# Row sums of the first triangle stage on ScalarE, and a new order of that stage's words

## The chip, the cores and the metric

The kernel runs on one core of a Trainium2 chip. A core has TensorE (PE, matrix products into PSUM; its weight loads are shown apart as PEld), VectorE (DVE), ScalarE (ACT), GpSimd (POOL) and SyncE (SP, which here only issues transfers). Each engine takes its instructions in program order and waits for semaphores of the others. The metric is the time on the device in microseconds (us); less is better. Two times of this kernel that lie within about 0.2% of each other can't be told apart.

## The reference, cut to what matters

```python
# x: 4 images of 64 x 64 x 256, fp32
f, g, v = xt @ Wf + bf, xt @ Wg + bg, xt @ Wh + bh          # layer 0: attention over 4096 positions
beta = softmax(einsum('bqd,bkd->bqk', g, f), axis=-1)
x = x + (einsum('bqk,bkd->bqd', beta, v) @ Wo + bo)
q, k, v1, v2 = (x @ W for W in (Wq, Wk, Wv1, Wv2))          # layer 1: triangle attention, 8 heads of 32
scores = einsum('bilhd,bljhd->biljh', q, k) / sqrt(32)
att = softmax(scores, axis=2)                               # over l
out = einsum('biljh,bilhd,bljhd->bijhd', att, v1, v2)
h = layer_norm(x + out @ Wo)
out = layer_norm(relu(h @ W1 + b1) @ W2 + b2 + h)
```

The change concerns one thing in it: for the first image, the denominators of the second softmax, which are sums of exp(scores) over l.

## The kernel before, in words

The four images go one after the other, each through an attention stage (`layer0`) and a triangle stage. For images 1 to 3 the triangle stage (`next_layer1`) also carries the layer norms and the MLP of the image before. For image 0 there is no image before, so its triangle stage (`first_layer1`) carries other work: the projections of x of the other three images (24 slices of 512 positions, class `Ahead`) and half of its own v1 and v2 projections (class `Late`). The change touches only this first triangle stage.

**A step.** The stage has 32 steps: 4 pairs of heads, and for each pair 8 groups of 8 rows i. `scores` and `take_scores` make, for a whole pair, the tile S of exp(scores), 128 partitions (head, j) by 64 rows i by 64 values l. Then, for each step:

- `sums` (L967 and L969 on DVE): the sum over l of each of the step's 8 rows of 64 values, one TENSOR_REDUCE of 128x512 into 8 columns of `dens`, and the reciprocal of these into `rd`.
- `weights` (L977, ACT): 8 multiplications of a row by its reciprocal, into `es`.
- `turn_weights` (L994, PE): four 128x128 transposes into a PSUM tile `att`. The 8 matrices of 128x64 that this gives are the step's 8 *products*.
- `copy_weights` (L1002, ACT): the last 2 or 3 of these 8 matrices into SBUF as `attP`, for GpSimd.
- `product` (L1042): `att` times v2, 128x2048 values. The last `npool(step)` products go to GpSimd (`Rp`, two buffers), the others to DVE, which reads `att` in PSUM (`R`, three buffers).
- `accumulate` (L1052, PE): sums a product over l with v1 as the weights, eight instructions of 128x512 in four column groups, into a PSUM tile `acc`. Only when it has run is the product's buffer free.
- `take` (L1062, ACT) copies `acc` out, and `store` (L1071, SP) issues eight transfers per step.
- `stationary` (L1021, ACT): v1 into the weight tile `wsel`, of which there are two.

**The order.** Nothing schedules this at run time: the order is written out by hand as a list of words, ORDER0, which is run through once for each *period* (11 periods, of which 1 to 9 hold products). One period does four steps. A word is a letter, the step within the four (and for some letters the product or half), and after the slash how many periods late it is: in period p, `R25/2` is product 5 of step 4(p-2)+2. The words: S sums, W weights, t and c transposes and copy for GpSimd, R product, A accumulate, T take (and store), V stationary; sp, sf scores; e, f exp of scores; v, u, g, a, b the projections for the other images (v and g on PE, u and a on ACT, b on DVE); m, n, o, p the own late projections (m and o on PE, n and p on ACT). A word only puts instructions into an engine's queue, so the list fixes the order on each engine, and the engines slip against each other as far as buffers allow.

A slice s of the projections ahead is loaded by SP (`xT`, L377) when both words v and g of slice s-2 have been issued. When four products of steps 24 to 29 have been issued, GpSimd issues transfers that spread gT and fT for the next image's attention (L278, L284).

`npool(step)` is 2 for every fourth step (step % 4 == 3) and 3 for the others: 11 of a period's 32 products for GpSimd, 88 of 256 in the stage.

Of the kernel before, what the change touches and what calls it, by code (L numbers as in the profile page):

```python
# [14 lines left out]
AF = mybir.ActivationFunctionType  # L15
ALU = mybir.AluOpType
AX = mybir.AxisListType
# [8 lines left out]
IG = 8  # L26
NIG = N // IG
# [37 lines left out]


ORDER0 = """
    A21/2 g1/2 S3/1 W1/1 A27/2 A23/2 A26/2 a1/2 V3/2 A24/2 R32/2 b1/2 m1/2 T20/2 c3/2 t0/1 v2/2 n1/2 R25/2 A25/2
    R33/2 sp0/1 T21/2 A32/2 R34/2 R36/2 R30/2 A33/2 e00/1 u2/2 e01/1 o1/2 R31/2 g2/2 c0/1 R37/2 A34/2 A36/2
    A30/2 A31/2 A37/2 V0/1 R35/2 T30/2 t1/1 R00/1 p1/2 a2/2 b2/2 A35/2 R03/1 T31/2 sf0/1 A00/1 R02/1 g0/1 f0/1  # L70
    a0/1 b0/1 R05/1 f1/1 R07/1 A05/1 A03/1 v3/2 R06/1 u3/2 m0/1 S2/1 W2/1 c1/1 v0/1 V1/1 R01/1 A02/1 n0/1 R04/1
    A07/1 A01/1 A04/1 R12/1 u0/1 A06/1 T00/1 sp1/1 T01/1 R13/1 R15/1 R14/1 A13/1 e10/1 e11/1 t2/1 R10/1 A12/1
    R17/1 V2/1 A15/1 A14/1 A10/1 R16/1 R11/1 S0 R22/1 W3/1 g3/2 c2/1 W0 A17/1 R27/1 A11/1 v1/1 R20/1 a3/2 b3/2
    u1/1 o0/1 p0/1 S1 R21/1 T10/1 t3/1 A16/1 T11/1 A20/1 R23/1 A22/1 R24/1 R26/1
""".split()


@with_exitstack
def attention_then_triangle_kernel(
# [6 lines left out]
    nc = tc.nc  # L86
# [22 lines left out]
    def ctile(shape, name):  # L109
        return const.tile(shape, F32, tag=name, name=name)  # L110
# [100 lines left out]
    dens = ctile([P, 256 + 16], "dens")  # L211
# [130 lines left out]
    class Ahead:  # L342
        def __init__(self):
            shapes = {"x": [C, T], "v": [P, NKC, P], "gf": [8, P, 2, 2, P]}
            self.d = {
                b: {n: dram.tile(sh, F32, tag="ah" + n, name="ah" + n, bufs=NB) for n, sh in shapes.items()}
                for b in range(1, NB)
            }
            self.n = 8 * (NB - 1)
            self.raw, self.xT, self.vp, self.gf, self.t = {}, {}, {}, {}, {}  # L350
            self.parts = None
# [532 lines left out]
    class Layer1:  # L884
        def __init__(self, b, io, safe):
            self.b, self.io, self.safe = b, io, safe

            self.aT = dram.tile([C, 2, N // 2, N], F32, tag="aT", name="aT")
            io["a"] = self.aT
            self.S, self.v2, self.qk, self.v1, self.att, self.ao = {}, {}, {}, {}, {}, {}  # L890
            self.R, self.begun, self.acc, self.rec, self.e = {}, {}, {}, {}, {}
            self.owed = lambda: None

# [57 lines left out]
                )  # L953


        def sums(self, step):
            pair, ig = divmod(step, NIG)
            rows = self.S[pair][:, ts(ig, IG), :]
            if self.safe:
                nmx = small.tile([P, IG], F32, tag="mxl", name="mxl")  # L960
                nc.vector.tensor_reduce(nmx, rows, AX.X, ALU.max, negate=True)
                den = small.tile([P, IG], F32, tag="den", name="den")
                for i in range(IG):
                    nc.scalar.activation(rows[:, i, :], rows[:, i, :], AF.Exp, bias=nmx[:, i : i + 1])
            else:
                den = dens[:, ts(step, IG)]
            nc.vector.tensor_reduce(den, rows, AX.X, ALU.add)  # L967
            rec = small.tile([P, IG], F32, tag="rd", name="rd")
            nc.vector.reciprocal(rec, den)  # L969
            self.rec[step] = (rows, rec)  # L970
# [8 lines left out]

        def npool(self, step):  # L980
            if self.b == 0:
                return 2 if step % 4 == 3 else 3
            return 3 - step % 2


# [431 lines left out]
    def step_words(L, fetched, stored, spread, late=None):  # L1417
        made, taken, sps = {}, {}, {}

        def do(w, step, m):  # L1420
            if not 0 <= step < NSTEP:
                return
            if w == "R":
                if step not in made:
                    made[step] = 0
                    L.begin(step)
                L.product(step, m)
                made[step] += 1
                if made[step] == 4:
                    spread(step)  # L1430
                if made[step] == 8:
                    if step == 1:
                        L.fetch_v2(1)
                    if step == NIG - 1 and late is not None:
                        L.fetch_v2(2, 2)
                        late.room = True
                        late.fetch()
                    elif step in (NIG - 1, 2 * NIG - 1):
                        L.fetch_v2((step + 1) // NIG + 1)
                    fetched(step + 1)  # L1440
            elif w == "A":
                L.accumulate(step, m)
            elif w == "T":
                L.take(step, m)
                taken[step] = taken.get(step, 0) + 1
                if taken[step] == 2:
                    L.store(step)
                    stored(step)
            elif step == 0:
                return  # L1450
            elif w == "S":
                L.sums(step)
            elif w == "W":
                L.weights(step)
            elif w == "V":
                L.stationary(step)
                L.fetch_v1(step + 2)
            elif w == "t":
                L.turn_weights(step)
            elif w == "c":  # L1460
                L.copy_weights(step)


        def scores(j):
            if 0 <= j < 12:
                L.scores(1 + j // 4, j % 4)
                sps[j] = L.sp
                if j % 4 == 3 and j // 4 + 2 < NPAIR:
                    L.fetch_qk(j // 4 + 2)

        def take_scores(j, half):
            if 0 <= j < 12:
                L.sp = sps[j]
                L.take_scores(half)

        L.fetch_v1(2)
        return do, scores, take_scores

    def words_of(order):
        for w in order:  # L1480
            w, late = (w.split("/") + ["0"])[:2]
            yield w, int(late)

    def first_layer1(L, ahead, F):
        used = {}

        def fetched(step):
            if 24 <= step < 31:
                ahead.fetch(F, 1, step)

        own = Late(L)
        step_word, scores, take_scores = step_words(
            L, fetched, lambda step: None, lambda step: ahead.spread(F, 1, step), own
        )

        def front_word(w, s, cc):
            if not 0 <= s < ahead.n:
                return
            if w in "vg":
                used[s] = used.get(s, 0) + 1  # L1500
            if w == "v":
                ahead.values(s)
            elif w == "u":
                ahead.valued(s)
            elif w == "g":
                ahead.factors(s)
            elif w == "a":
                ahead.factored(s)
            elif w == "b":
                ahead.parted(s)  # L1510
            if w in "vg" and used[s] == 2:
                ahead.load(s + 2)

        for period in range(NSTEP // 4 + 3):
            if period == 1:
                L.owed()
            for word, late in words_of(ORDER0):
                i, last = period - late, int(word[-1])
                if word[0:2] == "sp":
                    if 2 * i + last > 0:  # L1520
                        scores(2 * i + last)
                elif word[0] == "e":
                    if 2 * i + int(word[1]) > 0:
                        take_scores(2 * i + int(word[1]), last)
                elif word[0:2] == "sf":
                    if i == 0:
                        scores(0)
                elif word[0] == "f":
                    if i == 0:
                        take_scores(0, last)  # L1530
                elif word[0] in "RATSWVtc":
                    step_word(word[0], 4 * i + int(word[1]), last)
                elif word[0] in "mnop":
                    if 0 <= i < 4:
                        own.word(word[0], 2 * i + last)
                elif 0 <= i < 4 and int(word[1]) < 2:
                    front_word(word[0], 2 * i + int(word[1]), last)
                elif 4 <= i < 8:
                    front_word(word[0], 4 * i - 8 + int(word[1]), last)
        ahead.fetch(F, 1, NSTEP)  # L1540
# [193 lines left out]
```

## Time and profile before

| what | value |
|---|---|
| median of 3 runs | 3623.9 us (3619.18 to 3624.72) |
| profiled execution | 3623.49 us; span 3621.6 us |
| PE busy in the span | 3516.2 us, 97% |
| DVE busy | 2849.8 us, 79% |
| ACT busy | 1923.5 us, 53% |
| POOL busy | 1777.1 us, 49% |
| first triangle stage, from its first product to the next image's first scores on PE | 443.5 to 872.2 us of the span |

The page divides the span into 40 slices of 90.5 us, and gives the busy share of each engine in tenths; the first triangle stage is slices 5 to 9 or so, counted from 0. Groups of instructions are given with a line, an engine, what they write and read with the shapes, a count, and then the busy time, the mean length of one in ns, and the idle time just before them with what ended it.

### The profile page before, as it was taken

The page shows a single profiled execution, that of the slowest core. Times are in us where ns is not written, and L with a number is a line of the kernel's source. Part 1 is how long each engine was busy: PE and PEld are TensorE (multiplying, and loading weights), DVE is VectorE, ACT ScalarE, POOL GpSimd, SP SyncE. Part 2 cuts the span into 40 slices and gives each one's busy share as a digit, 9 for nine tenths or more (in the row PEclk, how much of TensorE's full clock was granted, in tenths as well). Part 3 has the DMA queues.
Part 4 walks back from the last instruction along what each step waited for, and adds up shares of the span by engine and source line. Part 5 has one row for each costly group of instructions (what it writes and reads, how often), then busy time and mean ns, then how long its engine had stood idle before and what let it go on. Part 6 is the DMA issues. An engine that isn't in the chain of part 4 may idle for free.

```text
span 3621.6 us, 58681 instructions
## 1 busy us (share of the span) xinstructions
PE 3516.2 (97%) x22218; PEld 1887.8 (52%) x22218; DVE 2849.8 (79%) x2662; ACT 1923.5 (53%) x4221; POOL 1777.1 (49%) x904
## 2 busy tenths in 40 slices
PE   9999999988999999999999999999999999999998
PEld 6555444434555555554455555555355555555477
DVE  4777499996555569999777749999787766999987
ACT  3444455544444366665444446666444446777655
POOL 5000099995000058899111118989611116999920
PEclk9999999999999999999999999999999999999999
DMA  9444555456111264426322254343633335441221
GB/s 174 137 132 125 138 151 133 126 132 139 47 50 50 81 153 102 108 62 114 96 95 88 82 141 117 83 104 79 131 93 99 96 108 142 96 94 49 66 69 57
DMA packets 509492, 374.37 MB, mean 103 GB/s; under 512 B 320080, under 2 KB 450896, under 8 KB 500368
## 3 DMA queue, kind: packets, MB, share of 16 engines
q1 hardware_dynamic: 460160, 343.56, 34.7%
q0 software_dynamic: 36160, 19.94, 5.5%
q10 hardware_dynamic: 12880, 7.01, 0.7%
q8 instruction: 178, 2.92, 0.3%
q14 instruction: 114, 0.93, 0.1%
HBM read 205.73 MB, written 164.63 MB: 102 GB/s over the span
## 4 chain that ended last, share of the span: by engine, by line
PE 68%; POOL 7%; DVE 6%; issue 4%; ACT 2%; DMA 0%; SPq 0%; ACTq 0%; DVEq 0%; POOLq 0%
PE o L590 18%; PE acc L1052 17%; PE proj L673 6%; POOL Rp L1042 6%; PE s L563 5%; PE mp L1303 5%; PE zp L1323 5%; PE sp L940 3%; DVE R L1042 3%; PE v1p L705 2%; PE hp L1160 2%; PE y L642 1%; PE att L994 1%; PE htp L1270 1%; PE hp L1166 0%
## 5 line engine op out<-in xcount | busy, mean ns | idle before, releaser
L1042 POOL TENSOR_TENSOR Rp<-attP,v 128x2048 f32<-128x2048 f32 x328 | 1491.3, 4579 | 410.4 <-ACT attP L1002 367.3
L1042 DVE TENSOR_TENSOR R<-att,v 128x2048 f32<-128x2048 f32 x696 | 1545.9, 2277 | 70.4 <-PE acc L1052 51.8
L590 PE MATMUL o<-e,v 128*128 128x512 f32 x2048 | 1043.7, 592 | 0.0
L575 ACT ACTIVATE e<-s 128x1024 f32<-128x1024 f32 x512 | 522.9, 1023 | 532.4 <-PE s L563 447.6
L597 DVE TENSOR_TENSOR esum<-esum,e 128x2048 f32<-128x2048 f32 x224 | 511.8, 2285 | 369.9 <-ACT e L575 367.9
L563 PE MATMUL s<-gT,fT 128*128 128x512 f32 x1024 | 786.5, 770 | 8.8 <-ACT e L575 4.7
L1052 PE MATMUL acc<-R,wsel 128*32 128x512 f32 x5568 | 705.4, 602 | 27.7 <-DVE R L1042 20.4
L590 PEld LDWEIGHTS o<-e,v 128*128 128x128 f32 x2048 | 388.3, 190 | 276.7 <-issue 233.8
L1062 ACT COPY ao<-acc 128x1024 f32<-128x1024 f32 x256 | 256.3, 1012 | 291.5 <-PE acc L1052 203.3
L1052 PE MATMUL acc<-Rp,wsel 128*32 128x512 f32 x2624 | 345.5, 598 | 22.3 <-POOL Rp L1042 21.6
L1052 PEld LDWEIGHTS acc<-R,wsel 128*32 128x32 f32 x5568 | 155.4, 110 | 397.6 <-issue 277.4
L1337 POOL TENSOR_TENSOR hz<-hz,log_bc 128x512 f32<-128x512 f32 x32 | 45.6, 1426 | 599.9 <-ACT hz L1247 599.9
L563 PEld LDWEIGHTS s<-gT,fT 128*128 128x128 f32 x1024 | 194.4, 190 | 245.0 <-issue 231.9
L977 ACT ACTIVATE es<-S,rd 128x64 f32<-128x64 f32 x1024 | 258.3, 337 | 15.0 <-DVE rd L969 13.1
L1231 POOL TENSOR_SCALAR nt<-mv 128x2 f32<-128x2 f32 (+1 forms) x49 | 9.4, 191 | 505.1 <-DVE mv L1186 500.0
L1303 PE MATMUL mp<-hT,w 128*128 128x256 f32 x1024 | 244.7, 384 | 1.7 <-ACT hT L1275 1.7
L1323 PE MATMUL zp<-w,hid 128*128 128x256 f32 x1024 | 240.0, 385 | 2.5 <-ACT hid L1312 2.1
L1323 PEld LDWEIGHTS zp<-w,hid 128*128 128x128 f32 x1024 | 187.9, 190 | 50.1 <-issue 14.7
L1303 PEld LDWEIGHTS mp<-hT,w 128*128 128x128 f32 x1024 | 185.2, 190 | 54.7 <-ACT attP L1002 12.6
L619 DVE RECIPROCAL rec<-den 128x512 f32<-128x512 f32 x32 | 107.4, 3357 | 126.5 <-PE den L615 121.2
L1052 PEld LDWEIGHTS acc<-Rp,wsel 128*32 128x32 f32 x2624 | 80.9, 110 | 210.1 <-issue 143.6
L950 ACT ACTIVATE S<-sp 128x512 f32<-128x512 f32 x128 | 131.4, 1092 | 77.9 <-PE sp L940 77.9
(195 smaller groups left out, 3699.0 us busy)
## 6 DMA issues: line engine op xcount, KB each, us to landing
v<-v2d SPq DMA_DIRECT2D x44, 512.0 KB
v1c<-v1d SPq DMA_DIRECT2D x128, 128.0 KB
aT<-ao SPq DMA_DIRECT2D x1024, 16.0 KB
A<-aT SPq DMA_DIRECT2D x256, 64.0 KB
hz<-raw SPq DMA_DIRECT2D x32, 512.0 KB
y<-yT SPq DMA_DIRECT2D x56, 256.0 KB
q<-st SPq DMA_DIRECT2D x56, 256.0 KB
k<-st SPq DMA_DIRECT2D x52, 256.0 KB
```

The source lines that it names most:

```text
L563: nc.tensor.matmul(s_ps[r // 2][:, r % 2, :], fT[tt][:, ts(r * 4 + n, P)], gT[qb // 4][:, ts(qb % 4, QB)], start=True, stop=not safe,)
L575: nc.scalar.activation(e[g][:, 2 * j : 2 * j + 2, :], s_ps[j], AF.Exp)
L590: nc.tensor.matmul(o_ps[qb], F.v[tt][:, r * 4 + n, :], es[:, r, :], start=(k == 0 and r == 0), stop=(k == 7 and r == 3),)
L597: nc.vector.tensor_tensor(esum[qb], esum[qb], es, ALU.add)
L673: nc.tensor.matmul(ps, w[:, cc, rows], y(qb, cc), start=(cc == 0), stop=(cc == 1))
L950: nc.scalar.activation(self.S[pair][:, :, l0 : l0 + 8].rearrange("p i l -> p l i"), sp[:, lh], AF.Copy if self.safe else AF.Exp,)
L977: nc.scalar.mul(e[:, i, :], rows[:, i, :], rec[:, i : i + 1])
L1042: eng.tensor_tensor(R, src.unsqueeze(1).to_broadcast([P, D, N]), v2[h], ALU.mult)
L1052: nc.tensor.matmul(acc[32 * c : 32 * c + 32, n % 2, :], w[:, n, c, 16 * h : 16 * h + 32], R[:, ts(c, 8), :].rearrange("p d j -> p (d j)"), ...
L1062: nc.scalar.copy(self.ao[step][:, ts(np, 2)].rearrange("p k d j -> p k (d j)"), self.acc[step][np])
L1303: nc.tensor.matmul(self.mp[:, fc % 2, :], w1_sb[:, cc, ts(fc, P)], self.hT[tt][:, cc, :], start=(cc == 0), stop=(cc == 1),)
L1323: nc.tensor.matmul(zp[:, n, :], self.hid[tt][:, fc, ts(n, P)], w2_sb[:, fc, :], start=(fc == 0), stop=(fc == 3 and tt not in self.hT2),)
```

## The change

ScalarE adds up the rows: for each step from 1 on there is a new word K (`row_sums`), which runs eight activations of 128x64, each of which writes a row of S back onto itself with the identity function and puts the sum of the row into its column of `dens`. For these steps `sums` keeps only the reciprocal; step 0 is still added up by DVE, inside `layer0`. The number of products that GpSimd takes is read from a string of 32 digits, one for each step, and comes to 85 in place of 88. ORDER0 is replaced by another list.

```diff
 ORDER0 = """
-    A21/2 g1/2 S3/1 W1/1 A27/2 A23/2 A26/2 a1/2 V3/2 A24/2 R32/2 b1/2 m1/2 T20/2 c3/2 t0/1 v2/2 n1/2 R25/2 A25/2
-    R33/2 sp0/1 T21/2 A32/2 R34/2 R36/2 R30/2 A33/2 e00/1 u2/2 e01/1 o1/2 R31/2 g2/2 c0/1 R37/2 A34/2 A36/2
-    A30/2 A31/2 A37/2 V0/1 R35/2 T30/2 t1/1 R00/1 p1/2 a2/2 b2/2 A35/2 R03/1 T31/2 sf0/1 A00/1 R02/1 g0/1 f0/1
-    a0/1 b0/1 R05/1 f1/1 R07/1 A05/1 A03/1 v3/2 R06/1 u3/2 m0/1 S2/1 W2/1 c1/1 v0/1 V1/1 R01/1 A02/1 n0/1 R04/1
-    A07/1 A01/1 A04/1 R12/1 u0/1 A06/1 T00/1 sp1/1 T01/1 R13/1 R15/1 R14/1 A13/1 e10/1 e11/1 t2/1 R10/1 A12/1
-    R17/1 V2/1 A15/1 A14/1 A10/1 R16/1 R11/1 S0 R22/1 W3/1 g3/2 c2/1 W0 A17/1 R27/1 A11/1 v1/1 R20/1 a3/2 b3/2
-    u1/1 o0/1 p0/1 S1 R21/1 T10/1 t3/1 A16/1 T11/1 A20/1 R23/1 A22/1 R24/1 R26/1
+    A14/2 u1/2 A25/2 A15/2 T11/2 R26/2 A24/2 S1/1 R21/2 u2/2 R27/2 t3/2 R22/2 c3/2 m1/2 S0/1 A26/2 W0/1 A22/2
+    g1/2 A21/2 R36/2 g2/2 R23/2 A27/2 a2/2 n1/2 A23/2 R20/2 R34/2 a1/2 T21/2 A20/2 V3/2 sp0/1 T20/2 e01/1 R35/2
+    b1/2 A34/2 A36/2 R37/2 R31/2 e00/1 V0/1 t0/1 o1/2 v3/2 A31/2 R33/2 R32/2 R30/2 b2/2 A35/2 c0/1 A33/2 A32/2
+    A37/2 A30/2 p1/2 W1/1 T31/2 T30/2 v0/1 R03/1 sf0/1 R02/1 t1/1 R05/1 V1/1 u3/2 A03/1 g3/2 f0/1 f1/1 A02/1
+    R07/1 A05/1 o0/1 R01/1 K2/1 R06/1 A07/1 A01/1 u0/1 R00/1 A00/1 c1/1 a3/2 K3/1 p0/1 T00/1 R04/1 S2/1 g0/1
+    W2/1 R11/1 A04/1 A06/1 b3/2 sp1/1 a0/1 R10/1 T01/1 e11/1 R16/1 t2/1 R17/1 b0/1 A11/1 A10/1 R12/1 e10/1 A16/1
+    V2/1 c2/1 R13/1 A12/1 m0/1 v2/1 R15/1 S3/1 K1 A17/1 R14/1 A13/1 v1/1 n0/1 R25/1 T10/1 W3/1 R24/1 K0
 """.split()
+ON_POOL = "33233233323333322333323323232323"
...
+        def row_sums(self, step):
+            pair, ig = divmod(step, NIG)
+            if not self.safe:
+                for i in range(IG):
+                    row = self.S[pair][:, ig * IG + i, :]
+                    nc.scalar.activation(
+                        row, row, AF.Identity, accum_out=dens[:, step * IG + i : step * IG + i + 1]
+                    )
+                self.summed.add(step)
...
-            nc.vector.tensor_reduce(den, rows, AX.X, ALU.add)
+            if step not in self.summed:
+                nc.vector.tensor_reduce(den, rows, AX.X, ALU.add)
...
         def npool(self, step):
             if self.b == 0:
-                return 2 if step % 4 == 3 else 3
+                return int(ON_POOL[step])
             return 3 - step % 2
...
+            elif w == "K":
+                L.row_sums(step)
```

More of the change, by code (lines that the diff above doesn't have):

```diff
@@ L67 @@
 ORDER0 = """
-    A21/2 g1/2 S3/1 W1/1 A27/2 A23/2 A26/2 a1/2 V3/2 A24/2 R32/2 b1/2 m1/2 T20/2 c3/2 t0/1 v2/2 n1/2 R25/2 A25/2
-    R33/2 sp0/1 T21/2 A32/2 R34/2 R36/2 R30/2 A33/2 e00/1 u2/2 e01/1 o1/2 R31/2 g2/2 c0/1 R37/2 A34/2 A36/2
-    A30/2 A31/2 A37/2 V0/1 R35/2 T30/2 t1/1 R00/1 p1/2 a2/2 b2/2 A35/2 R03/1 T31/2 sf0/1 A00/1 R02/1 g0/1 f0/1
-    a0/1 b0/1 R05/1 f1/1 R07/1 A05/1 A03/1 v3/2 R06/1 u3/2 m0/1 S2/1 W2/1 c1/1 v0/1 V1/1 R01/1 A02/1 n0/1 R04/1
-    A07/1 A01/1 A04/1 R12/1 u0/1 A06/1 T00/1 sp1/1 T01/1 R13/1 R15/1 R14/1 A13/1 e10/1 e11/1 t2/1 R10/1 A12/1
-    R17/1 V2/1 A15/1 A14/1 A10/1 R16/1 R11/1 S0 R22/1 W3/1 g3/2 c2/1 W0 A17/1 R27/1 A11/1 v1/1 R20/1 a3/2 b3/2
-    u1/1 o0/1 p0/1 S1 R21/1 T10/1 t3/1 A16/1 T11/1 A20/1 R23/1 A22/1 R24/1 R26/1
+    A14/2 u1/2 A25/2 A15/2 T11/2 R26/2 A24/2 S1/1 R21/2 u2/2 R27/2 t3/2 R22/2 c3/2 m1/2 S0/1 A26/2 W0/1 A22/2
[5 more added lines that the diff above has]
+    V2/1 c2/1 R13/1 A12/1 m0/1 v2/1 R15/1 S3/1 K1 A17/1 R14/1 A13/1 v1/1 n0/1 R25/1 T10/1 W3/1 R24/1 K0
 """.split()
+ON_POOL = "33233233323322333323323323232323"
 @with_exitstack
@@ L892, in __init__ @@
             self.owed = lambda: None
+            self.summed = set()
         def fetch_qk(self, pair, first=False):
@@ L1530, in first_layer1 @@
                         take_scores(0, last)
-                elif word[0] in "RATSWVtc":
+                elif word[0] in "RATKSWVtc":
                     step_word(word[0], 4 * i + int(word[1]), last)
```

## The prediction

> **What bounds the kernel now.** The table of busy time comes first. PE is busy for 97% of the whole span, but the change touches one stage only, the first triangle stage, and an average over all stages does not say who sets the pace there. So I cut that stage into its periods of four steps, which the scores' matmuls mark (they begin at 540.70, 591.94 and 643.17 us, so a period lasts 51.2 us), and read the busy time of each engine per period. Columns: from and to, length, then busy us and count of PE, PEld, DVE, ACT, POOL, then PE's granted clock and the DMA share.
>
> ```profile
> 530.30:581.50 51.20, 48.78 (x544) 22.79 (x536) 50.35 (x34) 28.91 (x75) 49.94 (x12) 1.00 0.51 139
> ...
> 735.50:787.00 51.50, 43.90 (x454) 19.49 (x455) 50.83 (x37) 23.61 (x71) 51.34 (x16) 0.97 0.55 124
> 787.00:838.00 51.00, 44.57 (x449) 18.54 (x446) 47.97 (x32) 22.39 (x61) 50.96 (x19) 0.90 0.92 175
> 838.00:872.00 34.00, 27.41 (x288) 13.62 (x284) 23.80 (x16) 10.78 (x21) 26.85 (x10) 0.95 0.53 121
> ```
>
> DVE and POOL are both busy for 98% of a period; they share the products and bound the stage together. ACT is busy for 56%. PE's 48.8 us contain modelled ends; by the starts in the timeline a product's eight matmuls take 0.86 us, transposes 0.59, v 1.87, g 0.87, m 1.72, o 1.87, scores 1.9, and 32 products, 4 transposes and two each of the others make 46.3 us.
>
> Next the groups of this stage, for the length of one instruction (window 450 to 900 us, shapes kept apart).
>
> ```profile
> L1042 POOL TENSOR_TENSOR Rp<-attP,v 128x2048 f32<-128x2048 f32 x87 | 395.1, 4582 | 16.4 <-PE acc L1052 6.8 <-ACT attP L1002 5.5 <-issue 2.1
> L1042 DVE TENSOR_TENSOR R<-att,v 128x2048 f32<-128x2048 f32 x166 | 368.6, 2273 | 15.0 <-PE acc L1052 11.5 <-ACT attP L1002 3.5
> L977 ACT ACTIVATE es<-S,rd 128x64 f32<-128x64 f32 x240 | 60.7, 340 | 12.9 <-DVE rd L969 12.7
> L967 DVE TENSOR_REDUCE dens<-S 128x8 f32<-128x512 f32 x29 | 19.6, 674 | 0.0
> ```
>
> In a row these overlap a little: seven DVE products take 15.42 us, so one starts every 2.20; six on POOL take 27.25, one every 4.54; a sum starts 0.71 before its reciprocal; eight `es` rows take 2.02, one every 0.24. Both engines' idle time is small, and its largest piece is at the end of the stage, which the timeline of DVE and then PE shows.
>
> ```profile
> 849.99 2.29 DVE L1042 TENSOR_TENSOR R<-att,v 128x2048 f32<-128x2048 f32 x1 [6.58 <-PE acc L1052]
> ```
> ```profile
> 843.10 3.85 PE L383 MATMUL vp<-wh,xT 128*128 128x128 f32 x16 [4.53 <-DMA xT<-ahx]
> ...
> 868.24 1.07 PE L1052 MATMUL acc<-R,wsel 128*32 128x512 f32 x8
> 869.23 2.05 PE L383 MATMUL vp<-wh,xT 128*128 128x128 f32 x16
> 871.21 0.65 PE L251 MATMUL gf<-xT,wg 128*32 128x128 f32 x16
> ```
>
> PE waits for a slice xT, the accumulates behind it are late, DVE finds no free buffer for 6.6 us. After the last accumulate PE still has a v and a g, 3 us, before the next attention's scores at 872.22.
>
> **What the Trainium skill says.** *GPSIMD Engine Reference*, Engine selection, has GpSimd about twice as slow as VectorE on elementwise operations of two inputs; the trace agrees (4582 against 2273 ns), so a product moved from POOL to DVE costs half of what it frees. *TensorE: Matmul & The Clock Gate*, What's actually happening: after some 3.4 us of idling PE runs at half clock. Here the v behind the 4.53 us wait takes 3.85 us, against 1.98 at other places, so a stall of PE costs about twice. The price of an activation is used below.
>
> **The change, part by part.**
>
> *Row sums leave DVE.* 31 TENSOR_REDUCE (steps 1 to 31) by 0.71 us: -22.0 us of DVE.
>
> *Fewer products on POOL.* The digits add up to 85, against 88: POOL -3 x 4.54 = -13.6 us, DVE +3 x 2.20 = +6.6. Net DVE -15.4, POOL -13.6. Both engines that bound the stage lose about 14 us, as they must if the stage is to get shorter. That is the ceiling of this part.
>
> *Unevenness.* It isn't given back evenly. From the two lists I add up each period's work, in us:
>
> | period | 1 | 2 | 3 | 4 | 5 | 6 | 7 | 8 | 9 |
> |---|---|---|---|---|---|---|---|---|---|
> | before, DVE | 36.8 | 50.6 | 50.6 | 50.6 | 50.6 | 51.6 | 51.6 | 49.9 | 14.8 |
> | before, POOL | 36.4 | 50 | 50 | 50 | 50 | 50 | 50 | 50 | 13.6 |
> | after, DVE | 27.3 | 47.7 | 47.7 | 49.9 | 47.7 | 48.8 | 51.0 | 51.0 | 21.4 |
> | after, POOL | 27.3 | 50 | 50 | 45.5 | 50 | 50 | 45.5 | 45.5 | 22.7 |
>
> If the two engines could not slip against each other, each period would cost the larger: 407.2 before, 402.3 after, a gain of 5. If they slip freely, POOL's 13.6. The slip needed is about 5 to 7 us; POOL has two buffers (one product ahead, 4.5 us), DVE three. I take the middle: -9.5.
>
> *Eight activations per step on ACT.* The trace has the form, but with 128x256:
>
> ```profile
> 1303.69 0.37 ACT L1201 ACTIVATE junk<-hp 128x256 f32<-128x256 f32 x1
> 1303.95 0.19 ACT L1201 ACTIVATION_READ_ACCUMULATOR junk<-hp 128x1 f32 x1
> 1304.04 0.47 ACT L1205 ACTIVATE junk<-hp,mv 128x256 f32<-128x256 f32 x1
> ```
>
> One row is two instructions and 0.35 us. With 64 elements it can't take longer; at the 0.833 ns per element of *ScalarE: Activation LUTs*, What ACT_TABLE_LOAD costs, 192 fewer save 0.16 us, an estimate, which leaves 0.19. So 1.5 to 2.8 us per step. I take 0.25, near the `es` row's pitch: 2.0 us per step, 62 us in the stage, 8 per period. ACT goes from 28.9 to 37 of some 50 us. It isn't the bound, and I cost it at nothing in the steady state: its idle time hides it. Were ACT late, T words would hold PE's `acc` tiles (two, shared with the scores), and through PE both DVE and POOL.
>
> *The new wait.* The reciprocal on DVE now waits for ACT's rows. Behind S2 in DVE's queue stand the products R11 and R10, behind S1 and S0 R21 and R22, behind S3 R14, and PE waits for these. By adding up the queues K2 is done about 29 us into a period and S2 due at 31.7; K3 31.5 against 43.3; K1 about 43 against 50; K0 about 50.3 against 54.6. The tightest has 2.7 us: nothing, unless a row takes the upper 0.35. At the stage's start there is no such lead: K1 stands behind the layer0's last weight copies on ACT (to 444.4), so S1, and behind it R03, waits until about 446.8, where the first product on DVE now starts at 443.51. That is +3.3; but before, DVE lost 2.2 and 2.0 us soon after (waits for gf and PE), and the new order has its first g later. I take +2 (0 to 3.3).
>
> *The order on PE.* What the list must do is put each accumulate A between its product's end and the start of the product that needs the buffer (three later on DVE, two on POOL). With the works above I laid PE's queue against DVE's over a period. The narrowest place: A21 comes at 8.3 behind m1 and g1 and should be over when R20 starts at 6.8, while A22 ahead of it can't start before R22's end; PE may run at most 2.1 us early. That costs about 0.5 us per period, no more than DVE idles per period now (0.7), so nothing.
>
> *Loads ahead.* Between the issue of a load of xT and its first use on PE there lie now, at the narrowest (slices 13, 17, 21), 3.6 us of PE's work, and the wait of 4.53 above is slice 21. In the new order the narrowest have 7.6. Nothing is behind that wait any more but a transfer of a few us; yet SP's queue carries the stores of T (8 in 5.0 us, 8.49 once) and the large loads of the next image there. Gain 0 to 4.5; I take -1.5. The spreads on POOL keep their count and place among the steps.
>
> *The tail.* v3 and g3 stood last in the old list; in the new one products and A30 are last and v3 and g3 go before, under the 20 us of DVE and POOL in period 9, where PE has only 20.6. The 3 us between the last A and the scores go: -3.
>
> Sum: -9.5 +2 -1.5 -3 = -12. The profiled execution's 3623.49 us (its span and 1.9 around it) stands 0.4 below the median, so nothing is to be corrected: 3611.5 us.
>
> **Rivals.** (a) *PE becomes the bound.* Periods 2 to 4 hold 46.3 us of PE at full pace and up to 48.8 with the gaps after each wait (a product after a wait takes about 1.0 us, not 0.86). The other two engines come down to 48 to 50, so hardly 1 us per period can be won, and the gain ends at about -5: 3618.5. For it: the 48.8; against it: from period 5 on PE has only 41 to 45. (b) *Slower: missed accumulates.* If the order leaves PE waiting for a POOL product with DVE's accumulates behind it, DVE and POOL lose in each of the eight periods. It decides at 13.6/8 = 1.7 us per period; at 3 us it gives 24 - 13.6 = +10.4, 3634. For it: A17, A06, A07 stand early against POOL (POOL's running ends lie 2 to 3 us behind PE's), and PE's waits fall to half clock beyond some us. Against: the list before has windows as narrow and idles by 0.7 to 1.3 us per period. (c) *ACT's row at 0.35 us*: 2.8 per step, S2 late by nothing to 1 us, four times per period at worst one of them: +8 in the stage, 3619.5. That the sums don't leave DVE can be excluded, since the built order has only reciprocals there.
>
> **How the numbers follow.** The forecast (3604 to 3616) gets 0.62, because both bound engines lose work and no queue that I added up is late; (a) and (c) together 0.13; (b) 0.25. What a measurement can tell from no change is about 0.2%, 7.2 us: faster is below 3616.6, slower above 3631.1. Of (a) and (c) 0.04 fall on the faster side and 0.09 within; (b) runs from 3624 to 3650, 0.05 of it within and 0.20 above. The forecast may miss its own range a little on either side without changing sign. So faster 0.66, same 0.14, slower 0.20. The range leaves out the far half of (b) and what lies below 3602: 3602 to 3634.
>
> **What would show it.** Right: the stage from 443.5 to about 860; periods of 49 to 50.5 us with DVE and POOL still over 95% busy; POOL 85 products; ACT at 37 of 50, a row sum at 0.25 us; no wait for xT over 2 us; first DVE product near 447. Wrong: idle time of DVE or POOL before L1042 above 25 us with PE acc as the releaser (b), PE without gaps in periods 2 to 4 (a), DVE waiting before the reciprocal for ACT in mid-period (c).

## The result, and the profile after

The changed kernel takes 3609.01 us in the median (3606.6 to 3611.02), beside 3619.56 us for the kernel before on the same chip: a ratio of 0.9968, 95% interval 0.9958 to 0.9978, or 8 to 15 us less. The forecast was 3611.5. One thing of the diff above has to be put right: its string of digits adds up to 86. The changed kernel has `33233233 23322333 23323323 23232323`, which is 85, the number that the prediction counts with and that the trace shows. The profiled execution has 3609.44 us and a span of 3607.6, against 3623.49 and 3621.6. In the changed file the lines have moved: product is L1059 (was L1042), accumulate L1069, the copy `ao` L1079, `copy_weights` L1019, reciprocal L986; the activation of `row_sums` is L967.

First the stage cut into the same windows as before (from and to, length, busy us and count of PE, PEld, DVE, ACT, POOL, PE's granted clock, DMA share).

```profile
530.30:581.50 51.20, 48.69 (x532) 23.02 (x532) 45.30 (x28) 35.37 (x136) 47.38 (x11) 0.97 0.53 142
...
735.50:787.00 51.50, 45.04 (x480) 19.86 (x468) 51.50 (x35) 33.77 (x141) 51.48 (x17) 1.00 0.55 124
787.00:838.00 51.00, 43.95 (x469) 19.79 (x472) 51.00 (x35) 29.38 (x107) 50.96 (x18) 1.00 0.89 210
```

Two opposite things stand here. In the late windows DVE is now as full as POOL (51.00 of 51.00; it was 47.97). In the early window both have become *emptier*, 45 and 47 of 51.2 us against 50 before. Four sums that DVE no longer makes are 2.8 us of this; for the rest, something makes both wait. ACT has gone from 28.9 to 35.4 there.

The groups of the stage, shapes kept apart (window 440 to 870 us; the idle time of 305.3 us behind attP lies before the stage):

```profile
L1059 POOL TENSOR_TENSOR Rp<-attP,v 128x2048 f32<-128x2048 f32 x85 | 386.2, 4587 | 322.3 <-ACT attP L1019 305.3 <-PE acc L1069 16.2 <-POOL Rp L1059 0.7
L1059 DVE TENSOR_TENSOR R<-att,v 128x2048 f32<-128x2048 f32 x171 | 380.1, 2276 | 16.0 <-PE acc L1069 14.4 <-issue 1.3
L967 ACT ACTIVATE S<-S 128x64 f32<-128x64 f32 x248 | 59.7, 245 | 0.4
L967 ACT ACTIVATION_READ_ACCUMULATOR S<-S 128x1 f32 x248 | 47.1, 190 | 0.0
```

POOL has 85 products for 88, which is 13.3 us less, and idles 17.0 us within the stage where it idled 16.4. A row of sums is two instructions that overlap (245 and 190 ns); one row starts 0.24 us after the other, 1.9 us per step.

The timeline of PE shows a wait that the kernel before did not have, and the tail:

```profile
532.81 3.65 PE L485 MATMUL v2p<-yb,wv 128*128 128x512 f32 x4 [3.95 <-DMA yb<-y]
...
855.90 1.07 PE L1069 MATMUL acc<-R,wsel 128*32 128x512 f32 x8
856.79 0.62 PE L255 MATMUL gf<-xT,wg 128*32 128x128 f32 x16
...
857.77 1.20 PE L567 MATMUL s<-gT,fT 128*128 128x512 f32 x4
```

The waits for xT are gone. In their place word m (the own v2 projection) waits for its slice `yb`, here and once more at 635.57 us, by 3.95 and 3.89; each time its matmuls then take 3.6 us instead of 2.0, as the Trainium skill's *TensorE: Matmul & The Clock Gate*, What's actually happening, has it of a PE that has idled for some 3.4 us. At the end v3 now goes before the last accumulates, but a g still stands behind them; the next scores begin at 857.77 against 872.22.

**Where the gain came from.** The second `ao` copy of steps 3, 7, 11 and so on can be read off ACT's timeline; it follows the last accumulates of its step in both lists. The attention stage ahead of it is not changed by any edit, and yet it ends up to 3.7 us earlier in one trace than in another. So the copies are counted from one point that all kernels share, the start of DVE's sum of step 0, as in these lines of the changed kernel and of e8 (an experiment below):

```profile
438.47 0.69 DVE L984 TENSOR_REDUCE dens<-S 128x8 f32<-128x512 f32 x1 [16.34 <-ACT S L955]
```
```profile
434.82 0.69 DVE L984 TENSOR_REDUCE dens<-S 128x8 f32<-128x512 f32 x1 [16.31 <-ACT S L955]
```

The first row has that start in us of the span, the others the us from there to the start of the copy (the columns after the first three are kernels of the experiments):

| up to step | before | after | sums on DVE (e8) | late digits 11 (e11) | m0 early (e7) |
|---|---|---|---|---|---|
| sum of step 0, in the span | 438.1 | 438.5 | 434.8 | 437.0 | 437.8 |
| 3 | 63.3 | 62.1 | 62.3 | 61.3 | 61.0 |
| 7 | 114.5 | 115.7 | 115.4 | 114.6 | 111.0 |
| 15 | 217.0 | 218.4 | 218.1 | 216.6 | 211.9 |
| 23 | 320.4 | 319.8 | 323.0 | 318.6 | 316.2 |
| 27 | 376.8 | 369.1 | 376.3 | 372.4 | 365.5 |
| 31 | 431.3 | 418.6 | 428.3 | 426.1 | 415.0 |
| next scores on PE | 434.2 | 419.3 | 429.1 | 426.8 | 415.7 |

Up to step 23 the change has gained 0.6 us, next to nothing. Of its 14.9 us until the next scores, 12.1 come in the last eight steps (110.9 us before, 98.8 after) and 2.1 in the tail. From the next scores to the end of the span both kernels take the same time within 0.5 us (2749.4 and 2749.9), so the whole gain lies in this stage. What is special about these eight steps stands in POOL's timeline, of the kernel before:

```profile
814.31 1.32 POOL L284 DMA_DIRECT2D fT<-ahgf  x2
815.64 13.61 POOL L1042 TENSOR_TENSOR Rp<-attP,v 128x2048 f32<-128x2048 f32 x3
829.19 1.32 POOL L284 DMA_DIRECT2D fT<-ahgf  x2
830.53 13.55 POOL L1042 TENSOR_TENSOR Rp<-attP,v 128x2048 f32<-128x2048 f32 x3
848.55 4.58 POOL L1042 TENSOR_TENSOR Rp<-attP,v 128x2048 f32<-128x2048 f32 x1 [4.47 <-PE acc L1052]
```

and of the changed one:

```profile
811.27 1.32 POOL L288 DMA_DIRECT2D fT<-ahgf  x2
812.61 13.63 POOL L1059 TENSOR_TENSOR Rp<-attP,v 128x2048 f32<-128x2048 f32 x3
826.16 1.32 POOL L288 DMA_DIRECT2D fT<-ahgf  x2
827.49 27.25 POOL L1059 TENSOR_TENSOR Rp<-attP,v 128x2048 f32<-128x2048 f32 x6
```

Between its products POOL issues the spreads of gT and fT, 1.32 us a pair. Steps 24 to 27 thus had 11 products, 50 us, and four pairs, 5.3, on POOL: 55.3 of the 56.4 us that they took. With the digits 2323 a product fewer is there. After the change POOL runs from 687.93 to 854.73 us without a gap.

### The profile page after: what moved, and what is told of

Read it like the earlier page. It is cut to its first block, busy times and chain, and to the rows that moved or that the text cites. A ratio compares the mean times of both kernels' runs of the same rounds, so it can differ in the third digit from the quotient of the medians.

```text
span 3607.6 us, 59214 instructions
## 1 busy us (share of the span) xinstructions
PE 3510.5 (97%) x22218; PEld 1889.2 (52%) x22218; DVE 2835.4 (79%) x2634; ACT 1982.7 (55%) x4717; POOL 1763.1 (49%) x901
## 4 chain that ended last, share of the span: by engine, by line
PE 82%; POOL 6%; DVE 4%; issue 4%; ACT 2%; DMA 1%; SPq 0%; ACTq 0%; DVEq 0%; POOLq 0%
PE o L594 24%; PE acc L1069 19%; PE proj L677 8%; PE s L567 7%; POOL Rp L1059 5%; PE mp L1320 5%; PE zp L1340 5%; PE sp L945 3%; PE v1p L709 2%; PE hp L1177 2%; DVE R L1059 2%; PE y L646 2%; PE att L1011 1%; PE v1p L447 1%; PE htp L1287 1%
## 5 line engine op out<-in xcount | busy, mean ns | idle before, releaser
L1059 POOL TENSOR_TENSOR Rp<-attP,v 128x2048 f32<-128x2048 f32 x325 | 1478.2, 4580 | 411.6 <-ACT attP L1019 362.5
L1059 DVE TENSOR_TENSOR R<-att,v 128x2048 f32<-128x2048 f32 x699 | 1553.0, 2278 | 67.4 <-PE acc L1069 53.5
L601 DVE TENSOR_TENSOR esum<-esum,e 128x2048 f32<-128x2048 f32 x224 | 511.9, 2285 | 369.9 <-ACT e L579 368.0
L1069 PE MATMUL acc<-R,wsel 128*32 128x512 f32 x5592 | 706.0, 601 | 15.9 <-DVE R L1059 12.5
L1079 ACT COPY ao<-acc 128x1024 f32<-128x1024 f32 x256 | 256.4, 1012 | 297.0 <-PE acc L1069 216.7
L1069 PE MATMUL acc<-Rp,wsel 128*32 128x512 f32 x2600 | 340.6, 595 | 23.7 <-POOL Rp L1059 23.1
L1069 PEld LDWEIGHTS acc<-R,wsel 128*32 128x32 f32 x5592 | 159.4, 110 | 370.5 <-issue 278.4
L1069 PEld LDWEIGHTS acc<-Rp,wsel 128*32 128x32 f32 x2600 | 79.6, 110 | 222.0 <-issue 152.6
```

The costliest lines, as they stand in the source:

```text
L601: nc.vector.tensor_tensor(esum[qb], esum[qb], es, ALU.add)
L1059: eng.tensor_tensor(R, src.unsqueeze(1).to_broadcast([P, D, N]), v2[h], ALU.mult)
L1069: nc.tensor.matmul(acc[32 * c : 32 * c + 32, n % 2, :], w[:, n, c, 16 * h : 16 * h + 32], R[:, ts(c, 8), :].rearrange("p d j -> p (d j)"), ...
L1079: nc.scalar.copy(self.ao[step][:, ts(np, 2)].rearrange("p k d j -> p k (d j)"), self.acc[step][np])
```

## The experiments

The theory to test: DVE and POOL bound the stage together, so the sums on ACT and the shorter share of POOL pay only together, and only with an order that fits. Rivals: one part alone carries the gain; ACT's new work costs something; PE is the bound.

### Order alone (e1)

```diff
-ON_POOL = "33233233323322333323323323232323"
+ON_POOL = "33323332333233323332333233323332"
...
             elif w == "K":
-                L.row_sums(step)
+                pass
```

The new list; sums stay on DVE, and GpSimd keeps its 88 products.

> The new order of words alone: all row sums on DVE again and 88 products on POOL, so that DVE and POOL have the work they had before the change. If the gain is the work taken from DVE and POOL, only the tail and the loads ahead are left of it: 2 to 5 us faster than before, near 3616. If the gain is the order, nearly all of it stays: 3609 to 3611.

Measured: 3640.43 us, ratio 1.0054 (1.004 to 1.0068), slower. The new list with the old division costs 19 us. By the `ao` copies four steps take 54 to 56 us in mid-stage instead of 51.2.

### Sums on ACT in the old order (e2)

```diff
-    a0/1 b0/1 R05/1 f1/1 R07/1 A05/1 A03/1 v3/2 R06/1 u3/2 m0/1 S2/1 W2/1 c1/1 v0/1 V1/1 R01/1 A02/1 n0/1 R04/1
+    a0/1 b0/1 K2/1 R05/1 f1/1 R07/1 A05/1 A03/1 v3/2 R06/1 u3/2 m0/1 S2/1 W2/1 c1/1 v0/1 V1/1 R01/1 A02/1 n0/1 R04/1
...
-    R17/1 V2/1 A15/1 A14/1 A10/1 R16/1 R11/1 S0 R22/1 W3/1 g3/2 c2/1 W0 A17/1 R27/1 A11/1 v1/1 R20/1 a3/2 b3/2
-    u1/1 o0/1 p0/1 S1 R21/1 T10/1 t3/1 A16/1 T11/1 A20/1 R23/1 A22/1 R24/1 R26/1
+    R17/1 V2/1 K0 A15/1 A14/1 A10/1 R16/1 R11/1 S0 R22/1 W3/1 g3/2 c2/1 W0 A17/1 R27/1 A11/1 v1/1 R20/1 a3/2 b3/2
+    u1/1 o0/1 p0/1 K1 S1 R21/1 T10/1 t3/1 A16/1 T11/1 A20/1 R23/1 A22/1 R24/1 K3 R26/1
```

The old list with K words put in, and 88 products.

> The row sums on ScalarE alone: the old order with four words K put into it, 88 products on POOL. DVE loses 22 us, POOL nothing. If DVE and POOL bound the stage together, POOL's 400 us hold its length: 0 to 4 us faster than before, 3616 to 3620. If DVE alone had set the pace, 10 us or more faster, below 3610. If the wait of the reciprocal for ScalarE costs, slower than before.

Measured: 3634.18 us, ratio 1.0031 (1.0021 to 1.0041). Its POOL timeline, at the start and in mid-stage:

```profile
461.56 4.53 POOL L1059 TENSOR_TENSOR Rp<-attP,v 128x2048 f32<-128x2048 f32 x1 [8.83 <-issue]
...
545.98 49.92 POOL L1059 TENSOR_TENSOR Rp<-attP,v 128x2048 f32<-128x2048 f32 x11 [1.16 <-PE acc L1069]
```

A period is 51.07 us for 51.2: DVE has lost its four sums per period and nothing follows, because POOL alone fills the period with its 11 products. The whole loss is at the start, where two K words stand ahead of the weights on ACT: step 3 is over at 512.5 us instead of 501.4, and from there to step 31 it takes 367.7 us, before 368.0. The loss is thus most likely one of where the K words were put (no run with them elsewhere was made); that the sums alone gain nothing isn't. Two of the nine runs stand at 3626.6 and 3626.9 us, apart from the others (3632.3 to 3636.3); the trace is of one of the others.

### The old division in the changed kernel (e3)

```diff
-ON_POOL = "33233233323322333323323323232323"
+ON_POOL = "33323332333233323332333233323332"
```

> The changed kernel with 88 products on POOL in the old pattern (11 in each period) in place of 85: POOL +13.6 us, DVE -6.6 us, order and row sums as changed. If POOL's total work carries the gain, the time rises by 8 to 13 us to 3617 to 3622. If the two engines can't slip against each other, so that the larger of the two in each period counts (as the prediction half assumed), only periods 4, 7, 8 and 1 change: +3 to +5 us, 3612 to 3614.

Measured: 3639.77 us, ratio 1.0053 (1.0039 to 1.0067): 30 us above the changed kernel, more than either side expected, and the time of e1, with or without the sums on DVE. Three products cannot cost that by their length. POOL's timeline:

```profile
505.87 22.72 POOL L1059 TENSOR_TENSOR Rp<-attP,v 128x2048 f32<-128x2048 f32 x5 [2.03 <-PE acc L1069]
529.88 22.68 POOL L1059 TENSOR_TENSOR Rp<-attP,v 128x2048 f32<-128x2048 f32 x5 [1.30 <-PE acc L1069]
```

and PE's between the two:

```profile
524.78 1.07 PE L1069 MATMUL acc<-R,wsel 128*32 128x512 f32 x8
528.64 1.92 PE L1069 MATMUL acc<-Rp,wsel 128*32 128x512 f32 x16 [2.80 <-POOL Rp L1059]
530.38 1.04 PE L1069 MATMUL acc<-R,wsel 128*32 128x512 f32 x8
```

The new list begins with A14, A25, A15, then R26. Where R25 is DVE's that fits. With the old division R15 and R25 are both POOL's in every period: PE waits 2.80 us for R25, and A15, which frees the buffer that R26 needs, stands behind A25. POOL waits, and DVE waits for the accumulates further back (2.77 and 2.69 us in its timeline). The period comes to 54.15 us. In the new string no group of four steps has a 3 for both step 1 and step 2; the old one always has. e11 below fits this: its string has 11 products in each of the last groups of four, but never a 3 for both, and POOL has no gap there. So the time hangs on list and digits together.

### Other digits in the old order (e10, e9)

e10 is the kernel before with this edit, e9 is e2 with the same string.

```diff
+ON_POOL = "33233233323333322333323323232323"
...
-                return 2 if step % 4 == 3 else 3
+                return int(ON_POOL[step])
```

Both were meant to have the digits of the changed kernel, and don't: their string has 3332 2333 for steps 12 to 19 where the changed kernel has 2233 3323, and it adds up to 86. For the other 24 steps the two strings are the same.

> The kernel before with nothing changed but the division: the old order, the sums on DVE, the new digits (85 products on GpSimd). If order and division belong together (the theory, from the kernels with the new order and the old digits, which cost 3 us per period), the old list mismatches the new digits too: some periods have GpSimd or DVE waiting for PE acc where the list has the A words elsewhere, and the time is 3628 to 3650. If a division acts by its count alone, GpSimd, which is busy for all but 1.3 us of a period, loses 13.6 us and DVE gains 6.6: 3610 to 3624.

> The old order with the row sums on ScalarE as before in this study (3634.2 us with 88 products), now with the new digits (85 products). Theory that order and division belong together: no gain over 3634, or a loss, 3630 to 3650. If the counts alone matter: both DVE (-15.4 us) and GpSimd (-13.6 us) are relieved, 3619 to 3624; then the new list would not be needed for the gain itself, only for the start of the stage.

Measured: e10 3662.57 us, ratio 1.012 (1.0105 to 1.0136); e9 3681.61 us, ratio 1.0175 (1.0161 to 1.0189). In e10 POOL waits 5.5 us in each of two early periods, for the weights `attP` of a next step:

```profile
530.38 49.88 POOL L1043 TENSOR_TENSOR Rp<-attP,v 128x2048 f32<-128x2048 f32 x11 [5.49 <-ACT attP L1003]
585.76 77.04 POOL L1043 TENSOR_TENSOR Rp<-attP,v 128x2048 f32<-128x2048 f32 x17 [5.50 <-ACT attP L1003]
```

Here, too, a division that the list was not made for lengthens POOL's period, to 55.4 us. Which word of the old list makes it late was not traced. The loss does not come from the eight steps with other digits alone: in e10, steps 4 to 11, which come before them, take 110.7 us instead of 102.5, and steps 20 to 31 take 181.4 instead of 163.0. So in these steps the changed kernel's digits do not suit the old order, and a reading by counts alone is out. What exactly the changed kernel's 85 cost in the old order was not measured. The combinations, as ratios to the kernel before:

| order | products on POOL | sums on DVE | sums on ACT |
|---|---|---|---|
| old | 88 | 1 (before) | 1.0031 (e2) |
| old | 86, other digits | 1.0120 (e10) | 1.0175 (e9) |
| new | 88 | 1.0054 (e1) | 1.0053 (e3) |
| new | 85 | 0.9994 (e8, next) | 0.9968 (after) |

### Sums back on DVE in the changed kernel (e8)

```diff
             elif w == "K":
-                L.row_sums(step)
+                pass
```

> The changed kernel, with its order and its 85 products on POOL in its own pattern, but all row sums on DVE again: DVE +22 us, ScalarE -53 us. If DVE's work is on the path in the new order, 14 to 22 us slower than the changed kernel: 3623 to 3631, and slower than before. If the new order and the 85 products carry the gain alone, within 3 us of 3609.

Measured: 3617.08 us, ratio 0.9994 (0.9986 to 1.0003): no different from before. So the sums on ACT are worth some 9 us in the changed kernel (the ratios differ by 0.0026, the stage in the profiles by 9.8 us), not the 14 and more that I expected. The table of copies shows where: up to step 15 the two kernels are level, although the first sums of e8 don't wait for ACT, and from there to step 31 e8 takes some 210 us, the changed one 200. In the last eight steps DVE has 22 products of 2.20 and four sums of 0.71 per four steps, 51.2 us. They take 53.4 and 52.0, and in the first of these stretches DVE is busy for 53.2 us and POOL for 50.6; without the sums they take 49.4 and 49.4. There DVE is the bound if it keeps the sums.

### Eleven products per period to the end (e11)

```diff
-ON_POOL = "33233233323322333323323323232323"
+ON_POOL = "33233233323322333323323332333233"
```

The changed kernel, with POOL's share of the last eight steps as large as before, in a pattern that fits the list.

> The changed kernel with GpSimd's products of the last eight steps at 11 per four steps, as before the change (3233 for the digits 2323, twice), so 87 in all; everything else stays. By the copies of acc the changed kernel had gained nothing up to step 23 (758.3 us there, 758.5 before) and 12.4 us in the last eight steps, where GpSimd also issues the spreads of gT and fT (1.33 us a pair). Theory: GpSimd with the spreads sets the pace there (11 x 4.54 + 4 to 5 = about 55 us for four steps before, 49.4 after), so this kernel loses most of the gain: each group of four back to 53.5 to 56 us, +8 to +12 us, 3617 to 3621. Rival: the gain there comes from elsewhere (the sums off DVE, the loads of xT earlier, the new list): +0 to +4, 3609 to 3613.

Measured: 3617.42 us, ratio 0.9986 (0.9979 to 0.9992); the changed kernel has 0.9968. Steps 24 to 27 take 53.8 and 28 to 31 53.7 us, 4.4 and 4.3 more, one product of POOL each. POOL's timeline has no gap:

```profile
789.09 18.15 POOL L1059 TENSOR_TENSOR Rp<-attP,v 128x2048 f32<-128x2048 f32 x4
807.20 1.33 POOL L282 DMA_DIRECT2D gT<-ahgf  x2
808.53 9.08 POOL L1059 TENSOR_TENSOR Rp<-attP,v 128x2048 f32<-128x2048 f32 x2
```

So 8.7 of the 12.1 us of these steps are the two products taken off POOL. The other 3.4 remain when they are put back. In the kernel before, POOL waited 4.47 us in these steps, behind PE's wait of 4.53 us for the xT of slice 21; the new list has no such wait, and that is the likely rest, though no run singles it out. The forecast of this run was a little high (+8 to +12; the ratios differ by 0.0018, 6.5 us), since this kernel came to step 23 1.2 us earlier.

### Every row summed twice (e5)

```diff
-                for i in range(IG):
+                for i in [*range(IG), *range(IG)]:
```

The second pass gives the same sums.

> The changed kernel with every K word run twice (16 activations with their accumulator reads in place of 8, the same sums written again): ScalarE +53 us in the stage, about 7 us per period, all else unchanged. If ScalarE's idle time hides the row sums, within 3 us of the changed kernel: 3607 to 3612. If ScalarE's queue is on the path (late copies of acc, late weights), 10 to 50 us slower than that.

Measured: 3616.38 us, ratio 0.999 (0.9983 to 0.9996). ACT's busy time between 443.5 and 872 us rises from 285.9 to 337.7 us, and 7 to 8 us of that come through (7.2 in the profiles, 0.0022 by the ratios): between the two expectations. Costing ACT's first 59 us at nothing is thus supported only roughly.

### The m words moved (e4, e7)

Two attempts on the wait for yb. SP's timeline of the changed kernel tells why it is there:

```profile
620.31 10.50 SPq L1088 DMA_DIRECT2D aT<-ao  x8
...
632.00 1.00 SPq L470 DMA_DIRECT2D yb<-y  x2
```

The load stands in SP's queue behind eight stores that keep SP for 10.50 us; PE's m at 635.57 is the one that waits. In the kernel before, the loads of yb stood behind these stores as well, but m came later:

```profile
517.96 10.98 SPq L1071 DMA_DIRECT2D aT<-ao  x8
...
530.21 0.88 SPq L466 DMA_DIRECT2D yb<-y  x2
```
```profile
537.04 1.98 PE L481 MATMUL v2p<-yb,wv 128*128 128x512 f32 x4
```

There 6.8 us lie between the load and its use. In the changed kernel PE is ready for m at 528.86, before the load is issued at 529.01. e4 lets PE come later; e7 moves m0 and n0 forward, so that the next load of yb is issued ahead of the stores.

e4:
```diff
-    ... R22/2 c3/2 m1/2 S0/1 A26/2 ...
-    ... A27/2 a2/2 n1/2 A23/2 ...
-    b1/2 A34/2 A36/2 R37/2 ...
+    ... R22/2 c3/2 S0/1 A26/2 ...
+    ... A27/2 a2/2 A23/2 ...
+    b1/2 A34/2 m1/2 A36/2 n1/2 R37/2 ...
```

> The changed kernel with the words m1 and n1 some 8 us of PE work later, so that PE no longer waits for the load of yb (3.9 us twice, after which DVE idles 5.9 and 4.9 us and POOL 3.8 and 5.6). If that wait is on the path, 5 to 9 us faster than the changed kernel: 3600 to 3604. If the engines catch up with it later, or another wait takes its place, within 2 us of 3609.

Measured: 3610.61 us, ratio 0.9973 (0.9963 to 0.9984), the same as the changed kernel. The waits for yb are gone, and step 11 is over 4.3 us earlier (160.6 against 164.9, counted as in the table); but the projections end later, and at step 16 DVE waits 10.3 us for the v2 of the next pair of heads, and all is given back.

e7:
```diff
-    ... T00/1 R04/1 S2/1 g0/1
+    ... T00/1 R04/1 S2/1 m0/1 g0/1
...
-    V2/1 c2/1 R13/1 A12/1 m0/1 v2/1 R15/1 S3/1 K1 A17/1 R14/1 A13/1 v1/1 n0/1 R25/1 ...
+    V2/1 n0/1 c2/1 R13/1 A12/1 v2/1 R15/1 S3/1 K1 A17/1 R14/1 A13/1 v1/1 R25/1 ...
```

> The changed kernel with the words m0 and n0 some 8 us of PE work earlier: the load of yb for the next slice then stands in SP's queue ahead of step 0's stores in place of behind them, and nothing of the chain to pair 2's v2 gets later. If the waits for yb (PE 3.9 us twice, DVE 5.9 and 4.9 us behind them) are on the path and only the later v2 took their place in the run with m1 moved, 5 to 9 us faster than the changed kernel: 3600 to 3604. If yet another wait takes their place, within 2 us of 3609.

Measured: 3603.79 us (3601.12 to 3604.83), ratio 0.9956 (0.9942 to 0.9969), the fastest of all, some 4 us below the changed kernel by the ratios. The two intervals overlap, but each of its five runs lies below each of the changed kernel's eight. In its POOL timeline

```profile
469.48 136.17 POOL L1059 TENSOR_TENSOR Rp<-attP,v 128x2048 f32<-128x2048 f32 x30 [0.63 <-PE acc L1069]
...
652.05 9.04 POOL L1059 TENSOR_TENSOR Rp<-attP,v 128x2048 f32<-128x2048 f32 x2 [5.59 <-DMA v1c<-v1d]
```

POOL runs through the places where it waited 3.8 and 5.6 us, and four steps take 49.9. By the table the gain, 3.6 us, is made by step 23. The largest wait left is at step 16; the profile names v1c, but products there wait for several loads, and whether it is v1 or v2 was not tried.

## Why the prediction was right, and where not

**What bounds the kernel** held: DVE and POOL together. Relieving DVE alone gains nothing (e2), the new list and digits with DVE's sums kept gain nothing (e8), both together do.

**Row sums leave DVE, fewer products on POOL** (-15.4 and -13.6): the counts and durations came as stated; POOL's products shrank by 13.3 us.

**Unevenness** is the step that failed, though it hit near the total. It took the middle between 5 and 13.6 because the two engines' loads don't fall period by period, and laid the gain evenly over the stage. (Its last row of larger values adds up to 401.9, not 402.3, which changes nothing.) Its table gave POOL 50 us in periods 7 and 8 before. Steps 24 to 27 and 28 to 31, which fall in periods 7 to 9, took 56.4 and 54.5: I had noted that the spreads keep their place and had left their time, 1.32 us a pair on POOL, out of the sum. The stage gained 12.1 in those eight steps, 8.7 of it shown by e11, and 0.6 in the 24 steps before. The table's DVE, 51.0 in both periods after, was too high as well; these steps took 49.4 and 49.4.

**Eight activations per step** were priced at 2.0 us and took 1.9; ACT stands at 34 to 37 us per four steps up to step 23, where I had 37. At nothing they may be costed a little low: in e5 as many again cost 7 to 8 us.

**The new wait** came as laid out: the reciprocal waits for ACT once, at the start, and the first product on DVE follows at 447.12 (said: near 447). Counted from the sum of step 0, that product starts 3.2 us later than in e8 (8.65 against 5.45), but by step 3 the delay is gone: 62.1 against 62.3 in e8 and 63.3 before. So the +2 was charged for a delay that is made good.

```profile
446.84 0.20 DVE L986 RECIPROCAL rd<-dens 128x8 f32<-128x8 f32 x1 [7.45 <-ACT S L967]
447.12 11.08 DVE L1059 TENSOR_TENSOR R<-att,v 128x2048 f32<-128x2048 f32 x5
```

**Loads ahead** was half right. No wait for xT is left (likely some 3.4 us, said 1.5). But I looked at xT only: the loads of yb for m stand in the same queue behind the stores, and two new waits of PE, 7.8 us together with slowed matmuls behind them, took some 4 us back (e7). They are why the early periods are uneven (53.6, 49.2 and 53.5 us from step 3 to 15; 49.9, 49.9 and 51.0 in e7) and DVE and POOL not over 95% busy there, as the forecast wanted.

**The tail** gave 2.1 for 3: v3 went ahead, one g did not.

In sum -14.9 to the next scores in the profile, and 8 to 15 us by the runs, against -12. That the total came so near is in part luck: +2 was charged for a wait that cost nothing in the end, the loads of xT gave more than was said, and the waits for yb, which I did not have in the sum, took that back. Of the rivals, (b), PE waiting for a POOL product with accumulates behind it, exists and costs the 3 us per period that I gave it, but only where digits and list don't fit (e1, e3); (a) and (c) did not come.

## What to carry to other kernels

Where two engines share a bound, ask period by period what else each one carries, transfers that it issues among it: but for 2 us of tail the gain was made where POOL had extra work, and hardly anywhere else. A hand-written order and the division of work that it was written for belong together; measured apart, the parts gained nothing or did harm. Count a kernel's stages from a point that no edit touches, since the stage ahead can end some us earlier or later in each trace. After a reorder, look at every load whose place in the queue has moved, not only at the one that was waiting before.

## What was not expected of the hardware

Eight stores of a step keep SP busy for 5.0 to 6.7 us as a rule, but for about 10 where they follow large loads: 10.98 and 10.46 us in the kernel before and 9.61 and 10.50 in the changed one behind those of q and k, and 10.33 and 10.14 at step 15, behind those of v2; in three more places it is 7.1 to 8.7. Neither this time nor the place of the yb loads behind it is new; new is that the m which needs them now comes some 7 us sooner after the load. And the penalty for a misfit is out of scale with the work that moves: three products more on POOL, 13.6 us of it, cost 30 us (e3).
